# One of four states' inputs in the middle layers made by TensorE in two column tiles

## The chip, the cores and the metric

The kernel runs on one core of a Trainium2 chip. The metric is the time of one execution in device microseconds, as the median of several runs. Five engines work side by side, each with its own queue, in order: TensorE (PE in the profile; PEld is its weight load), VectorE (DVE), ScalarE (ACT), GpSimd (POOL) and SyncE (SP), which here issues the DMA transfers.

## The reference, cut to what matters

The network has four layers on images of 48 x 48 pixels with 192 channels, batch 4. Each rests on a selective scan over the 2304 pixels of an image: every channel has 16 states, and each state follows

```python
def step(h, t):
    d_t, u_t, b_t, c_t = t
    h = jnp.exp(d_t[..., None] * A) * h + (d_t * u_t)[..., None] * b_t[:, None, :]
    return (h, jnp.sum(h * c_t[:, None, :], axis=-1))
```

The factor `exp(d*A)` is called the decay here, `d*u` is called du, and `du*B` is what enters a state. The first layer (layer 0) and the last have 384 channels within. The two middle layers have 192 channels and four scans for each image: by rows, by columns, and both backwards. Their sum goes through a norm and, in the first of the two, a gate and a projection.

## The kernel before, in words

An image is cut into 6 chunks of 384 pixels. A *job* is one chunk of one direction of one image. In the middle layers (`ScanPools` with `parts=2`, jobs of class `DirJob`) the 192 channels lie in 3 blocks i of 64; the upper 64 partitions hold the same channels again with the other 8 of the 16 states. So a block has 8 states to a partition, in 2 groups g of 4 (`NG`). A job has 6 groups, and the number of a group in its job is called its *slot* here: even slots have g = 0. There are 2 layers x 4 directions x 4 images x 6 chunks = 192 jobs, and 1152 groups. Here is one group's way:

- `decay` (line 437): ACT computes four decays a, of 384 pixels each, two groups ahead of the scan. The buffer for a is one of three, so it waits for the scan of the group before the one now scanning.
- `fetch` (422): SP loads the rows of B and C of this group from HBM, repeated over the partitions, into a tile `bcb`.
- `drive` (465): POOL multiplies delta and x to du (tile `dus`), once per block. `enter` (470): ACT copies it to PSUM.
- `carry` (455): POOL copies the last state of the chunk before into one extra column of `bcb`, so that a scan over several states at a stretch starts each of them from it. That is why a row has 385 elements (`W`).
- `scan` (475): one DVE multiply, du times B of all four states (`inputs<-du,bcb`, 4 x 385 = 1540 elements), and one DVE scan over them (`h<-a,inputs`).
- `weigh` (501): POOL copies the last states out (`state<-h`) and multiplies h by C.
- `reduce` (516): TensorE sums the states into `y` (matmul records `y<-h,sum`), the lower and the upper half of the partitions going to two column tiles of 64.
- `take` (568), `gate` (572), `close` (577): ACT copies y out, TensorE adds its halves (`ps<-yc,sum`), ACT copies the result to `o`, and SP stores it.

Layer 0 and the last layer (`MambaJob`, `parts=1`) already have the form that the change brings to the middle layers. There, of the four states of a group, two (`MADE`) are not multiplied by DVE: TensorE makes du*B. For this a job writes B of these states to HBM and from there, one element of 4 bytes at a time, on the diagonals of 128 x 128 squares of zeros (`spread`, 641, tensors `be` and `dg`); `fetch` (662) loads them as part of `bcb`; `turn` (685) transposes du on TensorE and ACT copies it to `duT`; and `fill` (710) multiplies duT by the diagonal squares into the PSUM tile `made`. DVE then scans the made states straight from there (`h<-a,state,made` in layer 0, each state from its carried value).

The order of all this is written out in `run_jobs` (1029). At step t it queues the scan of group t, the decays of t+2, the weighing of t, the work of the next job that is due at this slot (`stream.run`: the projection to B, C and delta's input at slot 1, the three deltas at slot 2), the turn of t+2 if that is a block's first group, side work (the norms of finished images, in one job of four), the gate of t-3 if that was a block's last group, the drive of t+3, and the reduction of t-`behind`. Last comes `fill` of t+1. `behind` is 2 where TensorE makes inputs and 1 in the middle layers:

```python
        if 0 <= t - behind < len(groups) and behind == 1:
            job, i, g = groups[t - behind]
            job.reduce(i, g)
        if t + 1 < len(groups):
            job, i, g = groups[t + 1]
            job.fill(i, g)
```

Operations of DVE, POOL and TensorE that go through `InOrder` (51) and those of ACT (`in_order`, 106) keep this order; most transfers of SP are not bound to it. PSUM has 8 banks. In the middle layers before: four for `inputs`, one for du, one for y and two for `ps`, a pool of two buffers that projections, deltas, gates and side work use in turn.

Of the kernel before, what the change touches and what calls it, by code (L numbers as in the profile page):

```python
# [13 lines left out]
AF = mybir.ActivationFunctionType  # L14
# [7 lines left out]
Q = 96  # L22
# [6 lines left out]
MADE = 2  # L29
LINE = 3 * MADE * 128  # L30

# [30 lines left out]
class K:  # L62
# [100 lines left out]
    def mean_weights(self, n):  # L163
        w = self.tile(self.const, [Q, Q], f"mean{n}")
        self.nc.vector.memset(w, 1.0 / n)
        return w
# [82 lines left out]
class ScanPools:  # L249
# [6 lines left out]
    def __init__(self, k, ctx, parts, rows):  # L256
# [6 lines left out]
        self.made = parts == 1  # L263
# [9 lines left out]
        self.given = NG - MADE if self.made else NG  # L273
# [7 lines left out]
        if self.made:  # L281
            self.made_inputs = k.tile(self.vec, [128, 1024], "made")[:, 512 - CH : 512 + CH]
            self.n_jobs = 0
            self.diags = []
            zeros = self.decays[2].rearrange("p j l -> p (j l)")[:, : LINE + 1]
            k.g.memset(zeros, 0.0)
            for n in range(2 * self.groups):
                d = k.dram([128 * (LINE + 1)], "dg")
                k.nc.sync.dma_start(d.rearrange("(t x) -> t x", x=LINE + 1), zeros)
                self.diags.append(d)  # L290
# [41 lines left out]
class ScanJob:  # L332
# [16 lines left out]
    def turn(self, i):  # L349
        pass  # L350

    def turn_back(self, i):
        pass

    def fill(self, i, g):
        pass
# [55 lines left out]
    def spread(self):  # L412

        self.bc = self.k.dram([2 * N, self.pools.W], "bc")
        self.k.nc.sync.dma_start(self.bc, self.bcd[: 2 * N, :])
# [6 lines left out]
    def fetch(self, g):  # L422

        k, pools = self.k, self.pools
        wide = pools.wide
        both = k.tile(pools.bcs, [128, 2, NG, pools.W], "bcb")
        self.bcb[g] = both[:, 0, :, :], both[:, 1, :, self.tokens]
        self.fetched[g] = []
        for m in range(pools.parts):
            at = (m * pools.groups + g) * 2 * NG  # L430
            ins = k.nc.sync.dma_start(
                both[m * wide : (m + 1) * wide].rearrange("p s j l -> p (s j l)"),
                self.bc[at : at + 2 * NG, :].rearrange("r l -> (r l)").partition_broadcast(wide),
            )
            self.fetched[g].append(ins)

# [37 lines left out]

    def scan(self, i, g):

        k, pools = self.k, self.pools
        b, du, W = pools.b, pools.du, pools.W
# [3 lines left out]
        if pools.n_h >= pools.hbufs:  # L482
# [4 lines left out]
        k.v.tensor_tensor(  # L487
            b, du.unsqueeze(1).to_broadcast([128, NG, W]), self.bcb[g][0], ALU.mult
        )
        step = -1 if self.rev else 1  # L490
        h = self.h[i, g] = k.tile(pools.hs, [128, NG, W], "h")
        k.v.tensor_tensor_scan(
            h.rearrange("p j l -> p (j l)")[:, ::step],
            self.a.pop((i, g)).rearrange("p j l -> p (j l)")[:, ::step],
            b.rearrange("p j l -> p (j l)")[:, ::step],
            0.0,
            ALU.mult,
            ALU.add,
        )
# [36 lines left out]
class DirJob(ScanJob):  # L536
# [40 lines left out]
    def close(self, i):  # L577
        if i == 0:
            self.o = self.k.tile(self.pools.two, [64, 3, CH], "o")
        self.k.copy(self.o[:, i, :], self.ys)  # L580
        if i == 2:
            self.k.nc.sync.dma_start(self.part(self.dst), self.o)
# [5 lines left out]
class MambaJob(ScanJob):  # L588
# [52 lines left out]
    def spread(self):  # L641

        k, pools = self.k, self.pools
        sync = k.nc.sync
        n = pools.groups * (pools.given + NG)
        self.bc = k.dram([n, pools.W], "bc")
        sync.dma_start(self.bc, self.bcd[:n, :])
        be = k.dram([pools.groups, MADE, CH], "be")
        sync.dma_start(be.rearrange("g e l -> (g e) l"), self.bcd[n : 2 * N, self.tokens])
        at = pools.n_jobs % 2 * pools.groups  # L650
        pools.n_jobs += 1
        self.lines = pools.diags[at : at + pools.groups]
        for g in range(pools.groups):
            line = self.lines[g].rearrange("(t x) -> t x", x=LINE + 1)[:, :LINE]
            line = line.rearrange("t (b e c) -> t b e c", b=3, c=128)
            for e in range(MADE):
                with k.nc.allow_non_contiguous_dma(reason="diagonal"):
                    sync.dma_start(
                        line[:, :, e, 0:1], be[g, e].rearrange("(b t v) -> t b v", t=128, v=1)
                    )  # L660

    def fetch(self, g):

        k, pools = self.k, self.pools
        rows = pools.given + NG
        n = rows * pools.W
        t = k.tile(pools.bcs, [128, n + LINE], "bcb")
        both = t[:, :n].rearrange("p (j l) -> p j l", l=pools.W)
        self.bcb[g] = (
            both[:, : pools.given, :],  # L670
            both[:, pools.given :, self.tokens],
            t[:, n:].rearrange("p (b e c) -> p b e c", b=3, c=128),
        )
        ins = k.nc.sync.dma_start(
            t[:, :n],
            self.bc[g * rows : (g + 1) * rows, :]
            .rearrange("r l -> (r l)")
            .partition_broadcast(128),
        )
        k.nc.sync.dma_start(  # L680
            t[:, n:], self.lines[g][: 128 * LINE].rearrange("(t x) -> t x", t=128)
        )
        self.fetched[g] = [ins]

    def turn(self, i):

        k, pools = self.k, self.pools
        ps = k.tile(pools.ps, [128, 512], "ps")[:, :CH]
        self.turned_over(ps, self.du[i])
        self.duT[i] = k.tile(pools.two, [128, CH], "duT")  # L690
        k.copy(self.duT[i], ps)
        self.xd = k.tile(pools.one, [128, CH], "xd")
        k.act(self.xd, self.xs[:, i, :], AF.Identity, scale=self.w.D[:, i, :])
# [15 lines left out]

    def fill(self, i, g):  # L710

        k, pools = self.k, self.pools
        for b in range(3):
            at = slice(b * 128, (b + 1) * 128)
            for e in range(MADE):
                k.t.matmul(
                    pools.made_inputs[:, e * CH : (e + 1) * CH][:, at],
                    self.duT[i][:, at],
                    self.bcb[g][2][:, b, e, :],
                    start=True,  # L720
                    stop=True,
                    skip_group_check=True,
                )

    def scan(self, i, g):

        k, pools = self.k, self.pools
        waits = self.waits.pop((i, g))
        if g == 0:
            waits.append(pools.entered)  # L730
        if pools.n_h >= pools.hbufs:
            of = pools.n_h - pools.hbufs
            waits += [pools.readers[of], pools.weighed[of]]
        pools.n_h += 1
        k.gather(waits)
        n = pools.given
        du = pools.du.unsqueeze(1).to_broadcast([128, n, pools.W])
# [1418 lines left out]
```

## Time and profile before

| what | us |
|---|---|
| median of three runs (18009.92 to 18019.33) | 18016.76 |
| the profiled execution's own time | 18024.41 |
| its span, first to last instruction | 18022.6 |
| middle layers: first multiply of 1540 elements to last scan | 6085 to 12137 |
| DVE busy in the whole span | 16418.0 (91%) |
| TensorE busy in the whole span | 16243.2 (90%) |
| mean granted TensorE clock | 0.921 |

A line of the groups names the engine, the operation, out<-in by the tiles of the program, the shapes and the count; after the bar come busy time in us and the mean of one in ns, and after the second bar the idle time of the engine just before them with what ended it. A line of the timeline starts with its start and its duration in us; what stands in square brackets is the engine's idle time before it and what ended that. Records of one kind in a row are merged. An fp32 matmul is two records, each with its weight load; a transpose is one. A line of the windows gives a stretch, its length, the busy time of PE, PEld, DVE, ACT and POOL, each with the instructions in it, then the granted TensorE clock (1.00 is full speed), the mean share of the 16 DMA engines and GB/s.

### The profile page before, as it was taken

To read this page: it belongs to the slowest core of one execution; us is meant where nothing else is said; L and a number is where in the kernel's file an instruction comes from. 1 tells how busy PE (TensorE), PEld (TensorE's weight loads), DVE (VectorE), ACT (ScalarE), POOL (GpSimd) and SP (SyncE) were. 2 spreads that over 40 slices of the span, in tenths; PEclk is the share of its full clock that TensorE was granted. 3 is DMA by queue.
4 is the path that set the end of the run, shared out by engine and by line. 5 is a ranking of instruction groups with operands and counts; after the bars stand their busy time and mean duration, and the time that the engine had idled before them with its cause. 6 is when DMAs were issued, how large, how long until landed. Compare 5 with 4: busy or idle time off the path is not lost. (4 is left out here: it accounts for less than half of the span.)

```text
span 18022.6 us, 313028 instructions
## 1 busy us (share of the span) xinstructions
PE 16243.2 (90%) x118512; PEld 10759.8 (60%) x118512; DVE 16418.0 (91%) x10747; ACT 13776.3 (76%) x25601; POOL 14149.0 (79%) x10862
## 2 busy tenths in 40 slices
PE   9999999999999777787777877878999999999999
PEld 7787787888885322222222222226888888888874
DVE  8899899999996799999999999996999999999992
ACT  7888888888885567777777777777888888888874
POOL 7877878878874488888888888876888888888880
PEclk9999999999999878788888887789999999999999
DMA  4343343333333466666666666663343343433431
GB/s 137 122 128 124 125 134 122 128 126 128 128 126 93 105 137 146 151 148 153 152 148 149 144 150 140 147 145 112 122 127 125 120 124 123 132 123 122 125 118 50
DMA packets 1229187, 2324.58 MB, mean 129 GB/s; under 512 B 704376, under 2 KB 962016, under 8 KB 1075232
## 3 DMA queue, kind: packets, MB, share of 16 engines
q1 hardware_dynamic: 1227680, 2304.55, 46.8%
q8 instruction: 938, 15.37, 0.4%
q14 instruction: 569, 4.66, 0.1%
HBM read 2105.57 MB, written 200.98 MB: 128 GB/s over the span
## 5 line engine op out<-in xcount | busy, mean ns | idle before, releaser
L59 POOL TENSOR_TENSOR h<-h,bcb 128x1536 f32<-128x1536 f32 x3456 | 11312.2, 3273 | 798.6 <-DVE h L59 499.1
L104 ACT ACTIVATE a<-delta,A 128x384 f32<-128x384 f32 (+1 forms) x13824 | 7377.6, 603 | 911.7 <-DVE h L59 901.2
L59 DVE TENSOR_TENSOR_SCAN h<-a,inputs 128x770 f32<-128x770 f32 (+2 forms) x3456 | 7915.9, 2290 | 146.5 <-DVE inputs L59 1.8
L59 DVE TENSOR_TENSOR inputs<-du,bcb 128x770 f32<-128x770 f32 (+2 forms) x3456 | 4256.4, 1232 | 287.2 <-POOL bcb L59 100.9
L59 PE MATMUL made<-bcb,duT 128*128 128x128 f32 x27648 | 3559.6, 279 | 172.1 <-DVE h L59 139.6
L59 PEld LDWEIGHTS y<-ident,h 128*128 128x128 f32 x27648 | 3119.8, 142 | 845.0 <-issue 485.7
L59 PE MATMUL y<-ident,h 128*128 128x128 f32 x27648 | 3508.5, 277 | 59.8 <-ACT yt L104 49.2
L59 PEld LDWEIGHTS made<-bcb,duT 128*128 128x128 f32 x27648 | 3341.4, 195 | 273.9 <-DVE h L59 178.7
L59 PE MATMUL y<-h,sum 128*64 128x384 f32 x9216 | 2661.7, 643 | 750.2 <-POOL h L59 547.4
L59 DVE TENSOR_TENSOR_SCAN h<-a,made 128x768 f32<-128x768 f32 (+1 forms) x1536 | 2343.2, 1536 | 263.2 <-PE made L59 256.4
L59 PEld LDWEIGHTS y<-h,sum 128*64 128x64 f32 x9216 | 848.7, 167 | 2175.9 <-issue 982.2
L59 DVE TENSOR_TENSOR_SCAN h<-a,state,made 128x384 f32<-128x384 f32 x1920 | 1827.8, 993 | 221.1 <-PE made L59 219.4
L59 POOL COPY state<-h 128x4 f32<-128x4 f32 x2304 | 434.4, 189 | 1908.5 <-DVE h L59 1879.5
L59 PE MATMUL ps<-bcd,dtT 12*128 12x384 f32 (+1 forms) x2304 | 1076.9, 580 | 245.1 <-ACT delta L104 240.2
L59 PE MATMUL ps<-u,inT 96*128 96x384 f32 x3456 | 1251.7, 489 | 38.8 <-DMA u<-xn_wh 27.1
L104 ACT ACTIVATE delta<-ps,vec 128x384 f32<-128x384 f32 x1152 | 636.4, 577 | 344.3 <-PE ps L59 338.2
L59 PEld LDWEIGHTS ps<-bcd,dtT 12*128 12x128 f32 (+1 forms) x2304 | 415.1, 206 | 808.8 <-ACT delta L104 487.3
L59 PE MATMUL ps<-yt,outT 128*96 128x384 f32 x2304 | 808.7, 488 | 0.4 <-POOL yt L59 0.4
L59 PE MATMUL ps<-xh,diag 32*32 32x192 f32 x32256 | 796.8, 324 | 4.0 <-ACT xc L104 2.3
L59 PEld LDWEIGHTS ps<-u,inT 96*128 96x128 f32 x3456 | 600.5, 191 | 304.0 <-issue 36.4
L104 ACT ACT_TABLE_LOAD x603 | 773.6, 1283 | 10.6
L101 ACT ACT_TABLE_LOAD x600 | 769.8, 1283 | 9.8 <-PEq L2146 0.7
(147 smaller groups left out, 15082.7 us busy)
## 6 DMA issues: line engine op xcount, KB each, us to landing
bcb<-bc SPq DMA_DIRECT2D x768, 770.0 KB
bcb<-bc SPq DMA_DIRECT2D x384, 1155.0 KB
bcb<-bc SPq DMA_DIRECT2D x384, 1152.0 KB
bcb<-dg SPq DMA_DIRECT2D x768, 384.0 KB
y<-o SPq DMA_DIRECT2D x192, 288.0 KB
xs<-xi_wh SPq DMA_DIRECT2D x96, 288.0 KB
xs<-xi_hw SPq DMA_DIRECT2D x96, 288.0 KB
added<-y SPq DMA_DIRECT2D x96, 288.0 KB
```

What stands on the lines that cost most here:

```text
L59: return lambda *a, **kw: self.tc.keep_in_program_order(op(*a, **kw))
L101: self.in_order(self.nc.scalar.preload_act_table_set(LOG_EXP))
L104: return self.in_order(self.nc.scalar.activation(out, in_, func, **kw))
```

## The change

In the middle layers DVE now multiplies three of a group's four states. TensorE makes the fourth: for each of three pixel blocks of 128 and each half m of the partitions, one matmul of duT (128 pixels x 64 channels) with that half's diagonal square, into the half's own column tile of `made`. DVE scans three states as before and then the fourth from `made`, with the carried state as the scan's first value. `spread`, `fetch`, `turn`, `fill` and `scan` move from `MambaJob` to the common class, and `MADE` becomes a table by `parts`. In PSUM `inputs` gives one bank to `made`. `o` gets one buffer instead of two, and the weights `mean96` move to the pool of the stage that uses them. `behind` stays 2 for the outer layers and 1 for the middle ones (`turned`). Rows of the projection are put in another order to match.

```diff
-MADE = 2
-LINE = 3 * MADE * 128
+MADE = {1: 2, 2: 1}
...
-        self.made = parts == 1
+        self.made = MADE[parts]
+        self.turned = parts == 1
+        self.line = 3 * self.made * parts * 128
...
-        self.given = NG - MADE if self.made else NG
+        self.given = NG - self.made
...
+        made = k.tile(self.vec, [128, 512 * self.made], "made")
...
     def spread(self):
...
+        self.bc = k.dram([n, pools.W], "bc")
+        sync.dma_start(self.bc, self.bcd[:n, :])
+        be = k.dram([parts, pools.groups, made, CH], "be")
+        sync.dma_start(be.rearrange("m g e l -> (m g e) l"), self.bcd[n : 2 * N, self.tokens])
...
+        for g in range(pools.groups):
...
+            for e in range(made):
+                for m in range(parts):
+                    with k.nc.allow_non_contiguous_dma(reason="diagonal"):
+                        sync.dma_start(
+                            line[:, :, e, m, 0:1],
+                            be[m, g, e].rearrange("(b t v) -> t b v", t=128, v=1),
+                        )
...
     def fetch(self, g):
...
+        k.nc.sync.dma_start(
+            t[:, n:], self.lines[g][: 128 * pools.line].rearrange("(t x) -> t x", t=128)
+        )
...
+    def turn(self, i):
+
+        k, pools = self.k, self.pools
+        wide = pools.wide
+        ps = k.tile(pools.ps, [128, 512], "ps")[:, : 3 * wide]
+        for b in range(3):
+            k.t.matmul(
+                ps[:, b * wide : (b + 1) * wide],
+                self.du[i][:wide, b * 128 : (b + 1) * 128],
+                k.ident[:wide, :wide],
+                start=True,
+                stop=True,
+                is_transpose=True,
+                skip_group_check=True,
+            )
+        self.duT[i] = k.tile(pools.two, [128, 3, wide], "duT")
+        k.copy(self.duT[i].rearrange("p b d -> p (b d)"), ps)
+
+    def fill(self, i, g):
+
+        k, pools = self.k, self.pools
+        wide = pools.wide
+        for b in range(3):
+            for e in range(pools.made):
+                at = e * CH + b * 128
+                for m in range(pools.parts):
+                    k.t.matmul(
+                        pools.made_inputs[m * wide : (m + 1) * wide, at : at + 128],
+                        self.duT[i][:, b, :],
+                        self.bcb[g][2][:, b, e, m, :],
+                        start=True,
+                        stop=True,
+                        skip_group_check=True,
+                    )
...
     def scan(self, i, g):
...
+        scan(slice(0, n), slice(0, pools.W), pools.b.rearrange("p j l -> p (j l)"))
+        if pools.rows:
+            scan(slice(n, NG), self.tokens, pools.made_inputs)
+            return
+        for e in range(pools.made):
+            at = g * NG + n + e
+            first = 0.0 if self.prev is None else self.prev.state[:, i, at : at + 1]
+            scan(
+                slice(n + e, n + e + 1),
+                self.tokens,
+                pools.made_inputs[:, e * CH : (e + 1) * CH],
+                first,
+            )
...
     def close(self, i):
         if i == 0:
-            self.o = self.k.tile(self.pools.two, [64, 3, CH], "o")
+            self.o = self.k.tile(self.pools.one, [64, 3, CH], "o")
...
-    behind = 2 if jobs[0].pools.made else 1
+    behind = 2 if jobs[0].pools.turned else 1
```

## The prediction

> **What bounds the kernel now.** I first split the page's span by stage. The widths of DVE's two costliest groups tell the layers apart: 1540 elements is only in the middle layers, whose first multiply starts at 6085 us and whose last scan ends at 12137. The groups of instructions with shapes kept apart, over the whole span (mean ns after the busy time):
>
> ```profile
> L59 DVE TENSOR_TENSOR_SCAN h<-a,inputs 128x1540 f32<-128x1540 f32 x1152 | 3871.8, 3361 | 43.9 <-DVE inputs L59 0.5
> L59 DVE TENSOR_TENSOR inputs<-du,bcb 128x1540 f32<-128x1540 f32 x1152 | 2039.1, 1770 | 121.0 <-POOL bcb L59 28.4 <-ACT a L104 20.8 <-ACT du L104 16.7
> L59 DVE TENSOR_TENSOR_SCAN h<-a,inputs 128x770 f32<-128x770 f32 x1152 | 2024.0, 1757 | 41.9
> L59 DVE TENSOR_TENSOR_SCAN h<-a,state,made 128x384 f32<-128x384 f32 x1920 | 1827.8, 993 | 221.1 <-PE made L59 219.4
> L59 DVE TENSOR_TENSOR inputs<-du,bcb 128x770 f32<-128x770 f32 x1152 | 1109.1, 963 | 108.5 <-POOL bcb L59 72.5 <-ACT a L104 35.0 <-DMA bcb<-bc 0.4
> ```
>
> The last three are layer 0, where two of four states are already made by TensorE. Then the stage's busy times (order PE, weight load, DVE, ACT, POOL; then granted clock, DMA share, GB/s):
>
> ```profile
> 6085.00:12137.00 6052.00, 4710.49 (x14794) 1606.17 (x14794) 5907.75 (x2304) 4399.31 (x8193) 5026.89 (x4282) 0.80 0.65 147
> ```
>
> DVE is busy for 5908 of 6052 us: it is the bound, at 5.20 us a group (its multiplies start at 9020.51, 9025.71, 9030.91). But TensorE, at 0.80 of its clock, has its work spread round waits, so last I read one job's timeline engine by engine. A job is six groups, "slots" 0 to 5; slot 2 starts at 9020.51:
>
> ```profile
> 9020.54 1.55 PE L59 MATMUL ps<-bcd,dtT 12*128 12x384 f32 x4
> 9024.59 1.64 PE L59 MATMUL ps<-bcd,dtT 12*128 12x384 f32 x2 [2.50 <-ACT delta L104]
> 9026.17 0.90 PE L59 MATMUL ps<-yc,sum 128*64 128x384 f32 x1
> ...
> 9026.87 3.39 PE L59 MATMUL y<-h,sum 128*64 128x384 f32 x7
> ```
> ```profile
> 9020.51 2.13 ACT L104 ACTIVATE a<-delta,A 128x384 f32<-128x384 f32 x4 [1.16 <-DVE h L59]
> 9022.66 1.28 ACT L104 ACT_TABLE_LOAD   x1
> 9023.96 1.05 ACT L104 ACTIVATE delta<-ps,vec 128x384 f32<-128x384 f32 x2
> 9026.27 0.58 ACT L104 ACTIVATE delta<-ps,vec 128x384 f32<-128x384 f32 x1 [1.26 <-PE ps L59]
> ```
> ```profile
> 9000.01 3.44 POOL L59 TENSOR_TENSOR h<-h,bcb 128x1536 f32<-128x1536 f32 x1
> 9003.42 1.00 POOL L59 TENSOR_TENSOR dus<-delta,xs 128x384 f32<-128x384 f32 x1
> ```
>
> The first two show slot 2: TensorE stands 2.50 us for ACT's deltas, and the reduction of slot 1's states ends only at 9030.26, 9.75 us after the slot began. The third is slot 4 (start 8999.71): the next du is there 4.71 us into the slot. Today all this hides: with four h buffers a late reduction stops nobody.
>
> **DVE's gain.** Per group, a multiply and a scan of 1540 become 1155, half way between the rows: (963+1770)/2 = 1367 ns and (1757+3361)/2 = 2559 ns. The made state's scan is new: 993 ns (row). The gap per instruction is (5.20-5.13)/2 = 0.035. New group: 1.367+2.559+0.993+0.105 = 5.024, saving 0.176; x1152 = 203 us. In 32 of 192 jobs there is no carried state; such a scan averages 935 in layer 0, so 192 x 0.058 = 11 us more. Gain 214 us, if the made values are never late.
>
> **What the made values wait for.** `fill(t+1)` writes the one `made` bank, so it can't start until DVE's last scan of t ends; and TensorE's queue, in order, holds it behind `turn`, `gate` and `reduce(t-1)`, since `behind` stays 1 here. DVE needs it at 5.02 + 1.37 + 2.56 + 0.07 = 9.02 us after slot t's start. If it is late, DVE stops at the made scan, and behind that stand the next group's multiply, POOL's weighing and ACT's decays (which want the freed buffer). Nothing gives the stall back.
>
> Durations: gate and reduce together 2.12 us at full clock (9000.36 to 9002.48), 4.09 at half (9026.17 to 9030.26). Turn: three transposes, 0.49 in layer 0, 0.8 at half clock. Fill: 12 records. Unoverlapped, layer 0's twelve take 1.50 us; if the two column tiles overlap, half, 0.75. Page "TensorEngine Tiling (Array Packing)", Theoretical Speedup, allows up to 2x for a side of 64. The row half agrees: eight half-width records of 384 take 1.51, four full-width (u,inT) 1.46. But weight loads of `y<-h,sum` are busy 848.7/9216 = 92 ns each, twelve make 1.1. I take 1.1 at full clock, 1.6 at half (ends 0.75 and 3.0).
>
> *Slots 0 and 4.* Turn is queued ahead of gate and waits for du: 4.71+0.05. At full clock +0.49+2.12+1.1 = 8.47, cover 0.55. At half clock +0.8+4.09+1.6 = 11.25, late by 2.2.
>
> *Slot 2.* PSUM's two `ps` buffers now also serve turn, so gate gets the third delta's buffer and waits for ACT to read it: 9026.85 instead of 9026.17, 6.34 into the slot. Then 4.09+1.6: 12.03, late by 3.0. At full clock (one job's third delta ended at 5.60): 5.60+2.12+1.1 = 8.82, just in time.
>
> So the clock decides. Page "TensorE: Matmul & The Clock Gate", Part 1 (HAM oscillation), says that only idle gaps above about 3.4 us throttle. By it the 2.50 us gap leaves TensorE at speed and the kernel gains 214 us. The trace differs (same columns as the stage's line; the clock is third from the end):
>
> ```profile
> 9022.10:9024.60 2.50, 0.01 (x1) 0.01 (x1) 2.47 (x2) 2.47 (x5) 2.50 (x3) 0.79 0.00 0
> 9024.60:9026.20 1.60, 1.60 (x4) 0.52 (x4) 1.56 (x2) 0.41 (x1) 1.14 (x4) 0.50 0.12 31
> 9026.20:9030.30 4.10, 4.07 (x11) 1.25 (x10) 4.07 (x2) 4.00 (x7) 3.38 (x2) 0.50 0.98 213
> ```
>
> Counted over all jobs, the clock 5 to 8 us into slot 2 averages 0.53 to 0.63, and the reduction ends at a median of 9.44, already past 9.02 before fill is added. I take the row: 9.44+0.68 for gate's buffer+1.6 = 11.7, late 2.7; with a few jobs at full clock 2.5. For slots 0 and 4 the clock there averages 0.85 to 0.97, but turn now stands ahead, so TensorE idles some 3 us first; I take half clock in 3 of 10: 0.3 x 2.2 = 0.66, two slots 1.3. In 48 jobs side work (four `ny,center` records, 1.53 us) goes ahead of gate in slots 0 and 4; it overdraws the 0.55 by 1.0, twice: 48x2x1.0/192 = 0.5 per job. Odd slots: no turn, weighing ends at 3.75, cover 2 us: none.
>
> Sum: (2.5+1.3+0.5) x 192 = 826 us lost, 214 gained: +612.
>
> **The other edits.** *ACT:* three duT copies a job, at most 0.49 each; ACT is busy 73%, in slot 2 it follows the deltas, off gate's path: 0. *SP:* per job five more issues before fetch (be, four scatters at 0.625, layer 0's `dg<-be`) and two `bcb<-dg` at 0.43. bc is issued near 3.8 us into slot 2 (9024.30); with be's landing and the scatters' (estimated 2.5 each) the fetch goes out about 12 us after slot 2 began, lands near 16.6, and POOL's carry of the next job wants it at about 18.8 (3.7 into slot 5). Cover 2 us: 0, else POOL stands with the weighing behind it. The loads of xs and the store of o, also SP's, have a slot to spare. *DMA:* 786 KB of lines a job in, 394 KB of B rows out, on 4.6 MB: share 0.65 to about 0.71; hidden. *o in one buffer:* stored from 8999.91, rewritten at 9007.73: covered. *POOL:* carry copies 3 columns, not 4: 0; its weighing takes 3.44 here but 2.91 in layer 0, for reasons the trace doesn't show: if the new tile brings it to 2.91, slots 0 and 4 gain 0.53 of cover, slot 2 nothing; I keep 3.44. *Zero lines, `mean96`:* once, under 5 us. Outer layers: same instructions.
>
> **Rivals and numbers.** The sum stands against the profiled span, 18022.6 us (its run 18024.4), which is 7.6 over the median 18016.8; +612 on the median gives 18629.
> - *Fill late, mainly in slot 2* (chance 0.78): 18090 to 19190. Low end: only slot 2, late by 1.5: 288-214 = +74. High end: slot 2 at 3.0, the others at 1.3 each, side 0.6: 6.2x192-214 = +976, and up to 190 for a late fetch or unoverlapped fills.
> - *The clock stays up* (0.12): fills keep TensorE busy through today's gaps, slot 2 meets 8.82, and 214 us come back, less some side work: about 17830. It decides once slot 2's clock is near 1.0. For it: layer 0, with fills, shows 0.98. Against: slot 2's gap is ACT's, and its 12-row matmuls before and after it didn't bring the clock back.
> - *Near even* (0.04): slot 2 late by about 1.1 and nothing else: 1.1x192-214 = -3, 18014.
> - *Half clock in all three even slots, fills unoverlapped* (0.06): 3x3.2x192-214 = +1630, 19650.
>
> The range, 18000 to 19200, takes in the first and third case and leaves out the other two, 0.18. Within 0.2%, 36 us, is what a measurement of this kernel can't tell from no change. Faster 0.12, same 0.04, slower 0.84.
>
> **What the profile will show.** Right: DVE idle before `h<-a,made` in the middle stage, released by PE `made`, about 800 us in all, most after slot 2; groups of 1367, 2559 and 993 ns. Wrong: little such idle time with slot 2's clock near 1.0; or the idle time released by a DMA or POOL; or weighing at 2.91.

## The result, and the profile after

The changed kernel takes 18808.8 us (median of four runs, 18785.98 to 18816.29) against 18016.18 us of the kernel before in the same session: ratio 1.0438, 95% interval 1.042 to 1.0456. It is 793 us slower; the forecast was 612 slower. All of it is in the middle layers: their stage, from the first multiply to the last scan, grew from 6052 to 6851 us.

The groups of DVE instructions inside that stage, changed kernel (busy us and mean ns after the bar, then idle time ahead of them and what ended it):

```profile
L58 DVE TENSOR_TENSOR_SCAN h<-a,inputs 128x1155 f32<-128x1155 f32 x1152 | 2948.3, 2559 | 43.4
L58 DVE TENSOR_TENSOR inputs<-du,bcb 128x1155 f32<-128x1155 f32 x1152 | 1573.0, 1365 | 355.2 <-POOL bcb L58 248.6 <-DMA bcb<-bc 73.1 <-POOL state L58 5.4
L58 DVE TENSOR_TENSOR_SCAN h<-a,state,made 128x384 f32<-128x384 f32 x960 | 962.0, 1002 | 721.2 <-PE made L58 720.3
L58 DVE TENSOR_TENSOR_SCAN h<-a,made 128x384 f32<-128x384 f32 x192 | 180.8, 942 | 191.2 <-PE made L58 190.7
```

The stage's line of busy times, same columns as before:

```profile
6085.00:12936.00 6851.00, 5556.16 (x30358) 2699.73 (x30359) 5562.19 (x3456) 4497.41 (x8766) 5026.88 (x4284) 0.86 0.63 141
```

DVE's largest wait in the stage, and TensorE's (what waited, what ended it; us in total, times, longest):

```profile
DVE h L58 <- PE made L58: 911.0, 542, 5.2
```
```profile
PE ps L58 <- POOL dus L58: 722.3, 311, 4.6
```

Three things are to be read here. DVE's own work fell from 5908 to 5562 us, and the granted clock of TensorE rose from 0.80 to 0.86; both speak for the change. But DVE now stands 911 us for the values that TensorE makes, which it never did in this stage before, and 322 us (248.6 + 73.1) for the rows of B, against 31 before; a wait put down to POOL's `bcb` is the carry, which itself waits for the load. The sum is -346 + 911 + 290 = +855. Other waits of DVE came to 39 us less than before, and gaps that no wait explains to 18 us less, which makes +798, against +799 measured for the stage. TensorE's 722 us are `turn` waiting for du, 295 us in slots 0 and 419 in slots 4, with gate, reduce and fill behind it in the queue.

One job shows both waits. TensorE's timeline in slot 2, which starts at 9057.98:

```profile
9063.59 0.40 PE L58 MATMUL ps<-ident,dus 64*128 64x64 f32 x3
9064.33 0.54 PE L58 MATMUL ps<-yc,sum 128*64 128x384 f32 x1 [0.34 <-ACT delta L103]
...
9065.89 0.64 PE L58 MATMUL made<-bcb,duT 128*64 128x128 f32 x2
9066.42 0.85 PE L58 MATMUL y<-h,sum 128*64 128x384 f32 x1
9067.06 1.49 PE L58 MATMUL made<-bcb,duT 128*64 128x128 f32 x10
```

and DVE's timeline over slots 2 and 3, and in slots 0 and 1 of the next job:

```profile
9061.85 0.99 DVE L58 TENSOR_TENSOR_SCAN h<-a,state,made 128x384 f32<-128x384 f32 x1
9063.01 1.36 DVE L58 TENSOR_TENSOR inputs<-du,bcb 128x1155 f32<-128x1155 f32 x1 [0.16 <-POOL bcb L58]
9064.41 2.56 DVE L58 TENSOR_TENSOR_SCAN h<-a,inputs 128x1155 f32<-128x1155 f32 x1
9068.60 1.01 DVE L58 TENSOR_TENSOR_SCAN h<-a,state,made 128x384 f32<-128x384 f32 x1 [1.64 <-PE made L58]
...
9080.07 1.37 DVE L58 TENSOR_TENSOR inputs<-du,bcb 128x1155 f32<-128x1155 f32 x1
...
9088.95 1.37 DVE L58 TENSOR_TENSOR inputs<-du,bcb 128x1155 f32<-128x1155 f32 x1 [3.94 <-DMA bcb<-bc]
```

The bank is free from 9062.84 (9061.85 + 0.99), but fill stands behind gate and reduce: its first two records start at 9065.89, while the last of reduce are still under way, its other ten at 9067.06, and it ends at 9068.55. DVE's made scan, due at 9066.96, starts 1.64 us late. Gate waits for ACT's third delta because turn has taken its `ps` buffer, and starts 6.35 us into the slot. The prediction had 6.34; over all jobs the median is 7.1. The granted clock falls just there:

```profile
9060.00:9064.50 4.50, 3.24 (x19) 1.50 (x16) 4.30 (x4) 3.94 (x7) 4.42 (x6) 1.00 0.04 3
9064.50:9069.00 4.50, 4.04 (x22) 2.16 (x20) 2.87 (x2) 4.47 (x8) 2.26 (x2) 0.62 0.60 141
```

The second wait, 3.94 us at 9088.95, comes from SP's queue in the same slot 2:

```profile
9063.57 0.54 SPq L414 DMA_DIRECT2D bc<-bcd  x1
9064.17 0.28 SPq L416 DMA_DIRECT2D be<-bcd  x1
...
9066.97 2.59 SPq L426 DMA_DIRECT2D dg<-be  x4
9069.67 1.20 SPq L451 DMA_DIRECT2D bcb<-bc  x2
...
9073.14 1.60 SPq L451 DMA_DIRECT2D bcb<-bc  x2
```

The first group's rows are issued at 9069.67, 11.7 us into slot 2 (predicted: about 12). The second group's are issued at 9073.14, behind them in one burst, and the wait for them ends at 9088.9: 16 us after issue, 31 us into the slot.

Over all jobs, by the medians of the trace's DMA packets, counted from the start of slot 2: the first load goes out at 9.1 us and the last packet of the second group's rows ends at 28.5; in the kernel before it was 5.4 and 23.3. In between 3.7 MB move in 18 us, against 3.9 MB in 18 us before. So the burst isn't larger than it was; it starts 3.7 us later.

Over all 192 jobs, the wait for made falls on the slot whose scan is late as follows: slot 0 69 us, slot 1 95, slot 2 51, slot 3 380, slot 4 82, slot 5 234. Of the 322 us for rows, 257 are in slot 1.

### The profile page after: what moved, and what is told of

The parts are those of the page before. It is cut to its first block, busy times and chain, and to the rows that moved or that the text cites. A ratio compares the mean times of both kernels' runs of the same rounds, so it can differ in the third digit from the quotient of the medians.

```text
span 18808.1 us, 347232 instructions
## 1 busy us (share of the span) xinstructions
PE 17085.5 (91%) x134064; PEld 11850.1 (63%) x134064; DVE 16069.9 (85%) x11899; ACT 13874.4 (74%) x26177; POOL 14145.6 (75%) x10863
## 5 line engine op out<-in xcount | busy, mean ns | idle before, releaser
L103 ACT ACTIVATE a<-delta,A 128x384 f32<-128x384 f32 (+1 forms) x13824 | 7373.6, 603 | 21.6 <-DVE h L58 12.4
L58 DVE TENSOR_TENSOR_SCAN h<-a,inputs 128x770 f32<-128x770 f32 (+2 forms) x3456 | 6993.1, 2023 | 146.0 <-DVE inputs L58 1.4
L58 PE MATMUL made<-bcb,duT 128*128 128x128 f32 (+1 forms) x41472 | 4906.6, 287 | 254.6 <-DVE h L58 140.4
L58 PEld LDWEIGHTS made<-bcb,duT 128*128 128x128 f32 (+1 forms) x41472 | 4428.4, 181 | 905.1 <-issue 534.1
L58 DVE TENSOR_TENSOR inputs<-du,bcb 128x770 f32<-128x770 f32 (+2 forms) x3456 | 3790.8, 1097 | 526.5 <-POOL bcb L58 319.9
L58 DVE TENSOR_TENSOR_SCAN h<-a,state,made 128x384 f32<-128x384 f32 x2880 | 2790.3, 996 | 941.9 <-PE made L58 939.7
L58 DVE TENSOR_TENSOR_SCAN h<-a,made 128x768 f32<-128x768 f32 (+1 forms) x1728 | 2524.6, 1470 | 445.0 <-PE made L58 437.6
L103 ACT ACTIVATE duT<-ps 128x384 f32<-128x384 f32 (+1 forms) x1152 | 469.9, 408 | 1692.4 <-PE ps L58 1691.1
L58 PE MATMUL ps<-ident,dus 64*128 64x64 f32 (+1 forms) x3456 | 538.8, 268 | 763.7 <-POOL dus L58 722.3
L58 PE MATMUL ps<-bcd,dtT 12*128 12x384 f32 (+1 forms) x2304 | 972.9, 529 | 136.6 <-ACT delta L103 132.1
L58 PEld LDWEIGHTS ps<-ident,dus 64*128 64x128 f32 (+1 forms) x3456 | 376.4, 148 | 982.2 <-POOL dus L58 820.9
```

What stands on the lines that cost most here:

```text
L58: return lambda *a, **kw: self.tc.keep_in_program_order(op(*a, **kw))
L103: return self.in_order(self.nc.scalar.activation(out, in_, func, **kw))
```

## The experiments

The theory to be tested: the loss is the order of TensorE's queue (fill stands behind gate and reduce) and, beside it, loads that are issued late behind the scatters. The rivals: the loss is TensorE's clock; the late loads come from a larger burst, or from something else ahead of them on SP's queue; TensorE is simply full. Ratios are against the kernel before on the same chip, with their 95% intervals.

**Fill ahead of gate and reduce.** In the middle layers fill(t+1) is issued right after the projections of the slot:

```diff
         stream.run(at if at < per - 1 else per)
+        if behind == 1 and t + 1 < len(groups):
+            job, i, g = groups[t + 1]
+            job.fill(i, g)
```

> Only TensorE's queue order in the middle layers changes: fill(t+1) stands right behind the next job's projections and deltas, ahead of turn, gate and reduce(t-1). Nothing else, and the same work. Theory Q (the made values are late because fill is queued last): fill can start when DVE's last scan of t ends, or in slot 2 when the third delta is through (about 5.7 us into the slot), and is due about 8.8: DVE's 907 us of waiting for made in the stage fall below 150, the waits on bcb stay near 320; about 18050 us. Rival K (the half clock alone makes the chain too slow, wherever fill stands): the waiting falls by less than half, and the time stays above 18350.

Measured: 18755.6 us, ratio 1.0415 (1.04 to 1.0431). DVE's waits in the stage, then ACT's:

```profile
DVE inputs L58 <- ACT du L103: 775.0, 348, 6.9
DVE inputs L58 <- POOL bcb L58: 205.5, 122, 4.5
...
DVE h L58 <- PE made L58: 63.3, 68, 1.9
```
```profile
ACT duT L103 <- PE ps L58: 1488.2, 569, 13.0
```

Made is no longer late, so the place was right; but the time came back as a wait for `du`. Fill waits for DVE to leave the bank, turn now stands behind fill, ACT's copy of duT waits for turn, and behind that copy stands `enter`, which hands du to DVE. The stall had moved, not gone, and the time is far from the 18,050 expected.

**No scatters.** Leaves out the copy to `be` and the four scatters of a job; the diagonals stay zero, so the fourth state receives nothing. The loads keep their bytes.

```diff
-        sync.dma_start(be.rearrange("m g e l -> (m g e) l"), self.bcd[n : 2 * N, self.tokens])
+        if parts == 1:
+            sync.dma_start(be.rearrange("m g e l -> (m g e) l"), self.bcd[n : 2 * N, self.tokens])
...
-        for g in range(pools.groups):
+        for g in range(pools.groups if parts == 1 else 0):
```

> Leaves out, in the middle layers, the store of the made rows (be) and the four scatters onto the diagonals, so that the lines stay zero and the fourth state of each group gets nothing; the loads of the lines and all of TensorE's work stay. Theory L (the new waits of DVE on bcb, 321 us in the stage against 31 before, come from the fetch that must wait for be and the scatters and then sends both groups' loads at once): those waits fall below 80, waits for made stay within 100 of 907; 18500 to 18560 us. Rival P (POOL's carry is late because the whole group chain is late): the waits on bcb stay above 250, time within 60 of 18809.

Measured: 18650.1 us, 1.0351 (1.0336 to 1.0367). DVE's waits:

```profile
DVE h L58 <- PE made L58: 992.5, 579, 6.7
DVE inputs L58 <- POOL bcb L58: 58.7, 165, 1.1
DVE inputs L58 <- DMA bcb<-bc: 23.9, 2, 22.4
```

The waits for rows fall from 322 to 83 us, so the scatter path makes the loads late: the first load goes out at 5.6 us into slot 2 instead of 9.1, and the second group's rows are there at 22.1 instead of 28.5 (medians). One thing more changed with it: with no scatter to wait for, the load of one group's diagonals goes out ahead of the burst. The time falls by 159, not 239: the waits for made grew by 81, as slack that the one stall gave was used up by the other.

**No fill.** Leaves out turn, the copy of duT and fill (`made` is set to zero once):

```diff
+        if parts == 2:
+            k.nc.vector.memset(made, 0.0)
...
     def turn(self, i):
+        if pools.parts == 2:
+            return
...
     def fill(self, i, g):
+        if pools.parts == 2:
+            return
```

> Leaves out turn, its copy and fill in the middle layers: made is set to zero once and the fourth state of each group gets nothing; DVE's instructions and the loads are those of the changed kernel. Measures what DVE gains alone. If a group costs DVE the 4.80 to 4.88 us from start to start that undisturbed groups of the changed kernel show, the stage comes to 1152 x 4.85 = 5590 us plus the waits on bcb (300): about 17850 us. If it were the 5.02 that I summed from the rows, about 18100 us. Theory L also expects the waits on bcb to stay (over 200 us); rival P expects them gone with the late made values (under 80).

Measured: 18248.5 us, 1.0131 (1.0114 to 1.0148). DVE's waits:

```profile
DVE inputs L58 <- POOL bcb L58: 467.0, 226, 5.7
DVE inputs L58 <- DMA bcb<-bc: 72.7, 24, 6.0
```

Even with TensorE's part gone the kernel is slower than before, and 400 us slower than the 17,850 expected. Late rows alone, 540 us where 300 were expected, are more than the 237 us between this kernel and the one before.

**Dummy matmuls to hold the clock up.** First into a spare part of `made` (six ahead of the third delta, ten ahead of turn in slots 0 and 4), then, since these waited for DVE on that tile, into the `ps` tile that is overwritten next (six ahead of the second delta, ten ahead of turn):

```diff
+    def keep_warm(self, ps, n):
+        for _ in range(n):
+            k.t.matmul(ps[:, :128], k.ident, k.ident, start=True, stop=True, skip_group_check=True)
...
+        if pools.parts == 2 and i != 2:
+            self.keep_warm(ps, 10)
```

> Adds matmuls that nobody reads: six before the third delta of a job (where TensorE waits for ACT in slot 2) and ten before turn in slots 0 and 4 (where it waits for du). Theory K (the half clock is what makes fill late): the clock of the stage rises from 0.86 to above 0.95, DVE's 907 us of waiting for made fall to 300 to 500; 18250 to 18450 us. Theory Q without the clock (order and waits for ACT decide, whatever the clock): waiting for made stays above 750 or rises, since the added matmuls stand in the same queue; 18750 us or more.

> The added matmuls once more, now into the ps tile that the next operation overwrites, so that they wait for nothing of DVE: six before the second delta, ten before turn in slots 0 and 4. Theory K (half clock makes fill late): clock of the stage above 0.94, waiting for made from 907 to 300 to 550, 18250 to 18500 us. Theory Q (order and the waits for ACT and POOL, whatever the clock): waiting for made stays above 750, 18650 us or more.

Measured: 19363.5 us, 1.0751 (1.0735 to 1.0767), for the first: its waits for made are 1668 us, because the dummies, which share a tile with fill, stood waiting for DVE (571 us of TensorE's time ahead of work on `made`, 6 in the changed kernel); it tells nothing of the clock. For the second: 18836.6 us, 1.0455 (1.0439 to 1.047). Its stage line and its first wait:

```profile
6085.00:12947.00 6862.00, 6227.22 (x40307) 3699.06 (x40309) 5565.85 (x3456) 4493.98 (x8777) 5029.79 (x4284) 0.94 0.63 141
```
```profile
DVE h L58 <- PE made L58: 1063.1, 622, 4.3
```

The clock rose from 0.86 to 0.94. From gate to the end of fill it took a median of 2.8 us instead of 4.5 in slot 2 and 2.8 instead of 4.1 in slot 4. But gate started later, behind the dummies (8.1 instead of 7.1 us into slot 2, 7.6 instead of 5.4 into slot 4), fill ended later too (11.3 instead of 10.9, 10.4 instead of 9.7), and the time didn't fall. A higher clock bought with work in the same queue is worth nothing here; what a higher clock at no cost would give stays open.

**Turn, fill, gate, reduce.** As the first experiment, but with turn kept ahead of fill in TensorE's queue:

```diff
         if soon := at_group(t + 2, 0):
             soon[0].turn(soon[1])
+        if behind == 1 and t + 1 < len(groups):
+            job, i, g = groups[t + 1]
+            job.fill(i, g)
```

> Only TensorE's queue order changes again: turn, then fill(t+1), then gate and reduce(t-1). In the run with fill ahead of turn, DVE's waiting for made was gone, but ACT stood at its copy duT behind that fill, and DVE then waited 777 us for ACT's du. Theory Q: with turn in front, duT is copied about 5.3 us into an even slot and fill is through by 6.2 (slot 2: 8.1), due 8.8: waiting for made below 120, for ACT's du below 120, and the waits on bcb stay at 300 to 540 (the run without fill had 540): 18200 to 18350 us. Rival K (half clock): in slot 2 fill still ends after 8.8 in most jobs, waiting for made above 300, 18450 us or more.

Measured: 18560.5 us, 1.0303 (1.0285 to 1.032), the fastest so far of those that compute everything, and short of what was expected. DVE's waits:

```profile
DVE inputs L58 <- ACT du L103: 470.6, 277, 4.6
DVE inputs L58 <- POOL bcb L58: 261.3, 192, 4.8
DVE h L58 <- PE made L58: 106.7, 99, 3.9
```
```profile
PE made L58 <- DMA bcb<-dg: 429.2, 179, 6.6
```

The waits for du fall to 471 us only, 178 of them in slots 2 and 274 in slots 4. The last line is TensorE's, and new with fill moved up: in slots 0 and 1 it now stands 429 us for the load of the diagonals, the last of the late burst (436 us in the first experiment, 82 in the changed kernel). It is not what makes du late: in the 129 jobs in which TensorE stood over 0.3 us for the diagonals, DVE waits 2.6 us a job for du, in the other 63 2.2.

**The zero column by ACT.** The column of zeros at the entry of `bcd` was set by POOL, whose queue held a weighing ahead of it; ACT writes it instead, alone and together with the order just described:

```diff
-                k.g.memset(self.bcd[:, self.entry : self.entry + 1], 0.0)
+                e = self.bcd[:, self.entry : self.entry + 1]
+                if pools.parts == 2:
+                    k.act(e, px[:, 0:1], AF.Copy, scale=0.0)
```

> The changed kernel with ACT instead of POOL writing the zero column of bcd in the middle layers, nothing else. Theory L: waits on bcb fall from 321 to below 120, but the waits for made rise by about 100 as they did without the scatter (the stall that is taken away upstream is partly met again at made): about 18640 us. Rival B: 18780 us or more.

> As the order turn, fill, gate, reduce, and ACT instead of POOL writes the zero column of bcd in the middle layers (bcd times 0, one column), so that SP's store of bc no longer waits for POOL's weighing and the be, scatter and fetch chain starts about 4 us sooner. Theory L (late start of the fetch): the waits on bcb fall below 120, the group comes near the 4.85 us of DVE: 17700 to 17850 us, faster than both kernels. Rival B (bandwidth: the 390 KB more per job are the cause, not the start): waits on bcb stay above 250, 18000 us or more.

Measured: alone 18794.5 us, 1.0434 (1.0418 to 1.0449); with the order 18557.4, 1.0303 (1.0287 to 1.0318), the same as without it. The waits for rows stay at 251 and 306 us (322 and 320 without the edit). POOL's zero was not what made the loads late.

**Turn one group before its use.** Turn is issued in the odd slots, where du is two slots old, and fill behind it:

```diff
-        if soon := at_group(t + 2, 0):
-            soon[0].turn(soon[1])
+        if soon := at_group(t + behind, 0):
+            if t or behind == 2:
+                soon[0].turn(soon[1])
+        if behind == 1 and t + 1 < len(groups):
+            job, i, g = groups[t + 1]
+            job.fill(i, g)
```

> In the middle layers the turn is issued one group ahead of its use and not two: in slots 1, 3 and 5, where du was made two slots earlier, so nothing on TensorE, or on ScalarE's copy of duT behind it, waits for GpSimd; the fill follows the turn at once, ahead of gate and reduce. Theory Q (the loss is work standing in the wrong order, and each earlier reordering only moved the stall to ScalarE's copy of duT): waits for made stay near 110 us, those for du fall from 471 to below 150, those of late loads stay at 300 to 450; the time falls from the 18,560 of the order turn, fill, gate, reduce to 18,150 to 18,300. Rival K (what counts is the clock that TensorE gets and the work added to it): waits for du go elsewhere, time stays within 1% of 18,560.

Measured: 18704.4 us, 1.0392 (1.0372 to 1.0411), slower than with turn two groups ahead. TensorE's waits and DVE's:

```profile
PE made L58 <- ACT duT L103: 562.1, 457, 4.6
PE made L58 <- DMA bcb<-dg: 465.5, 151, 12.1
```
```profile
DVE inputs L58 <- ACT du L103: 573.5, 273, 5.2
DVE inputs L58 <- POOL bcb L58: 278.1, 178, 5.4
DVE h L58 <- PE made L58: 169.3, 183, 4.2
```

Now TensorE, at fill, stands for ACT's copy of duT and nearly as long for the diagonals, and gate and reduce stand behind fill; ACT's `enter` is late as before, presumably because gate's result comes late to ACT in its turn; that last link was read from the order and not tried. A third place for the same stall. The expectation had counted only POOL and TensorE and had left out that turn directly ahead of fill puts ACT's queue between them.

**Scatters straight from SBUF.** On top of that, without the copy to `be`:

```diff
-                            be[m, g, e].rearrange("(b t v) -> t b v", t=128, v=1),
+                            self.bcd[row : row + 1, self.tokens].rearrange("o (b t) -> o b t", t=128),
```

> As e10_turn_odd, and the four scatters of a job read the fourth state's rows straight from the tile in SBUF: the copy to be and the wait of about 2.2 us for its landing are gone from the queue of SyncE in the middle layers, the rows and the scatters are the same. Theory L (the second group's rows come late because the loads are issued late, behind the wait and the scatters): the waits of late loads fall by half, from 300 to 450 to about 150, and the time by 150 to 250 us against e10_turn_odd, which could bring it near or just below the kernel before (17,950 to 18,150). Rival B (they are late because the burst of loads itself is larger by the diagonals' tiles): no difference over 60 us from e10_turn_odd.

Measured: 19111.6 us, 1.0609 (1.0594 to 1.0625), 407 us slower than its base. SP's instructions on the diagonals, ns min/median/max, in this kernel and then in the changed kernel:

```profile
L436 SPq DMA_DIRECT2D dg<-bcd x764: 722/1263/2586, 6099.1 to 13176.9; - x191
```
```profile
L426 SPq DMA_DIRECT2D dg<-be x788: 530/624/1709, 6107.4 to 13197.9; - x197
```

An issue of a scatter whose source is a row in one partition of SBUF holds SP for 1.26 us, twice the 0.62 from HBM. The edit also takes the elements in another order, so source and order aren't told apart. The wait for `be` was gone: the scatters begin at 5.1 us into slot 2 instead of 8.8 (medians). But they end at 11.2, where they ended at 11.4; the first load goes out at 11.4 instead of 10.1, the second group's rows are there at 29.8 instead of 27.6, and the waits for rows rose from 345 to 621 us. The idea that a shorter path to the scatters brings the loads forward stands untested by this run, since the path was not shorter.

**No fill and no scatters.** Leaves out both, with the edits of those two runs together; DVE's three instructions and all loads stay.

> Leaves out in the middle layers both the turn, the copy of duT and the fill (made's tile is set to zero once) and the copy to be with the scatters (the diagonals' lines stay zero); VectorE's three instructions and all loads stay. It gives what VectorE alone gains. With the gain of 0.35 to 0.40 us per group that undisturbed groups show (4.8 against 5.2), 1152 groups give 17,580 to 17,620 plus what late loads are left; the prediction's 0.176 us per group would give 17,810. Expected 17,650 to 17,750. If late loads stay over 200 us without any scatter, the rival B of the larger burst holds, and the time is near 17,900.

Measured: 17671.6 us, 0.9813 (0.9798 to 0.9827), as expected. Stage line and DVE's waits:

```profile
6085.00:11804.00 5719.00, 4560.23 (x14802) 1573.64 (x14803) 5506.24 (x3456) 4366.51 (x8192) 5013.44 (x4283) 0.82 0.72 168
```
```profile
DVE inputs L58 <- POOL bcb L58: 53.8, 130, 2.0
```

This is what the change gives on DVE when next to nothing that feeds it is late: 340 us. Beside the run without fill alone, the copy to `be` and the scatters ahead of the loads cost 577 us, and the waits for rows fall from 540 to 55 us. The first load goes out at 5.6 us into slot 2 instead of 8.2, and the second group's rows are there at 21.6 instead of 26.3 (medians). So 2.6 of these 4.7 us are the later start. The other 2 are a longer burst, since here too one load of diagonals goes out ahead of it (16.1 us from first issue to last packet, against 18.2). The scatters as the cause are shown; the burst is not cleared by this pair of runs, but by the kernel before, where it was as long.

**Half of the reduce.** The order turn, fill, gate, reduce, with a reduce that sums only two of a group's four states (the other two are left out of the output), to take from TensorE about what turn and fill gave it:

```diff
-        for j in range(NG):
+        for j in range(2 * g, 2 * g + 2) if parts == 2 else range(NG):
```

> As e7_turn_fill (order turn, fill, gate, reduce), and the reduce of the middle layers sums two of a group's four states (two matmuls of 384 columns in the place of four; the other two states are left out of the sum). That takes some 1.2 us of TensorE per group (two records at the 0.57 to 0.61 us that they are busy in the profile), about what turn and fill added (1.4 us). Theory C (TensorE is simply full: after the change it is busy 4.81 us per group at a granted clock of 0.85, and VectorE needs 4.80, so each order only chooses who waits): the waits for made and du, 585 us together in e7_turn_fill, fall below 200, and the time from 18,560 to 17,950 to 18,150, with late loads of 250 to 350 us left. Rival O (the order of ScalarE's and TensorE's queues, waits on single instructions at fixed places): the waits stay above 400, the time above 18,350.

Measured: 18642.0 us, 1.0352 (1.0335 to 1.0369): not faster than its base of 18560.5 but slower by 0.4%. TensorE's groups in the stage, this kernel and then its base, and DVE's waits in this kernel:

```profile
L58 PE MATMUL y<-h,sum 128*64 128x384 f32 x4604 | 1867.0, 646 | 69.6 <-ACT yc L103 68.4
L58 PE MATMUL made<-bcb,duT 128*64 128x128 f32 x13824 | 1461.8, 348 | 795.4 <-DMA bcb<-dg 398.0 <-DVE h L58 266.5 <-ACT a L103 43.5
```
```profile
L58 PE MATMUL y<-h,sum 128*64 128x384 f32 x9202 | 2452.5, 565 | 75.3 <-ACT yc L103 73.5
L58 PE MATMUL made<-bcb,duT 128*64 128x128 f32 x13812 | 1231.3, 308 | 768.2 <-DMA bcb<-dg 429.2 <-DVE h L58 214.4 <-ACT a L103 55.1
```
```profile
DVE inputs L58 <- ACT du L103: 422.8, 262, 6.6
DVE inputs L58 <- POOL bcb L58: 275.0, 187, 5.5
DVE h L58 <- PE made L58: 184.5, 156, 5.5
```

Half of the reduce's records are gone, but its busy time falls only from 2452 to 1867 us, and the records got longer (reduce 565 to 646 ns, fill 308 to 348): the granted clock fell from 0.88 to 0.77 in the stage. The test was weaker than meant, since TensorE's busy time fell by 3% only (5387 to 5231 us). Still, 4600 matmul records fewer moved no wait away (607 us for du and made, 577 before): no sign that the amount of TensorE's work decides, though with the lower clock the rival isn't ruled out.

## Why the prediction was right, and which terms were off

The direction and the main mechanism were right: made values come late, because fill is queued last, and that costs more than DVE gains. The measured 18808.8 lies in the range and in the likeliest case's own range. The total is nearer than its terms: a gain that was too small and a loss put at nothing offset each other in part, which is luck. By its steps:

- **DVE's gain** was mis-sized. The rows were right to 1% (1367, 2559 and 993 ns forecast; 1365, 2559 and 1002 or 942 measured), but the sum of a group, 5.024 us, was not: the prediction added three gaps of 0.035 us, read where each instruction needs what the one before it uses. The multiply and the scan of one `inputs` tile keep that gap. But a made scan behind the scan of `inputs` needs nothing of it, nor does the next multiply need the made scan, and both start before the other's end. In the job shown, the scan at 9059.38 lasts 2.56, and the made scan starts at 9061.85, 0.09 ahead of its end. Undisturbed groups take 4.79 us. Layer 0 of the kernel before shows the same overlaps (3002.51 + 1.76 is 3004.27, and 3004.19 + 1.89 is 3006.08):

```profile
3002.51 1.76 DVE L59 TENSOR_TENSOR_SCAN h<-a,inputs 128x770 f32<-128x770 f32 x1
3004.19 1.89 DVE L59 TENSOR_TENSOR_SCAN h<-a,state,made 128x384 f32<-128x384 f32 x2
3006.01 0.96 DVE L59 TENSOR_TENSOR inputs<-du,bcb 128x770 f32<-128x770 f32 x1
```

  DVE's busy time shows a gain of 402 us without late made values (5908 to 5506, no fill and no scatters), of which 340 reach the kernel's time, and 346 in the changed kernel, where late scans lose the overlap; forecast 214.
- **Fill late**, forecast 826 us, measured 911. For slot 2 (whose late scan is slot 3's) 480 was forecast and 380 measured; for slots 0 and 4 with the side work 346 and 329, of which slot 4 has 234. The remaining 202 us come from the fills of the odd slots, to which the prediction gave no loss ("cover 2 us: none").
- **Fetch late**, put at 0 for a cover of 2 us, measured about 290 us more than before. This is the step that failed. Its time of issue fits the job shown (11.7 against about 12 us into slot 2; the median is 9.1). But it gave the first load 4.6 us to land, where 10 us pass from issue to last packet already in the kernel before (medians, 5.4 to 15.3). And it left out the second group's rows, which go out behind the first's and land last; DVE stands for them in slot 1. With the same step "*DMA:* hidden" fails: the mean share of 0.65 hides that the engines are full during the burst (1.00 from 9031.8 to 9046.0 in the kernel before).
- **"So the clock decides"** is not supported. The prediction took half clock in slot 2, and 0.85 to 0.97 in slots 0 and 4 with half in 3 of 10. In the changed kernel the means over all jobs, 5 to 8 us into the slot, are 0.72 to 0.92 in slot 2, 0.62 to 0.76 in slot 4 and 0.78 to 0.83 in slot 0. The stage's clock rose to 0.86 and the kernel is slower; with 0.94, bought by dummies, it is no faster, and with 0.77 (half of the reduce) only 0.4% slower than at 0.88. Fill ahead of gate and reduce took the waits for made from 911 to 63 us at a clock of 0.89, so the order decides who waits. The Trainium skill, "TensorE: Matmul & The Clock Gate", Part 1 (HAM oscillation), gives as its rule that TensorE should have no idle gaps above about 3.4 us. This case's trace differs: in the middle layers of the kernel before, the clock fell from full to half 359 times, and in 311 of them TensorE's longest idle time in the 4 us before was shorter than that. So the row was the better guide, and weighing it against the page led to the right side; that the clock was the cause is not shown by it.
- **Terms at nothing.** *ACT's duT copies:* right in this order (2 us of waits for du); with fill moved up, waits for du become the longest (775, 471 and 574 us). *POOL's weighing:* 3.44 kept, 3.45 measured. *o in one buffer:* "covered" was not quite so; ACT stood 91 us for the store (48 times), with nothing on DVE put down to it.
- **The last rival's sum** is too small by its own terms: with fills of 3.0 at half clock the even slots would be late by 3.6, 4.4 and 3.6 us, not by 3.2 each. It didn't come, since two column tiles overlap.

The balance of causes: fill gone alone gives 560 us (18808.8 to 18248.5), scatters gone alone 159, both 1137. The two stalls hide one another, so neither alone shows its price.

What stays open: whether a second `made` bank would end the chain DVE, fill, DVE. The kernel's eight banks of PSUM are taken (three for `inputs`, one each for du, `made` and y, two for `ps`), and it wasn't tried. Nor was another queue for the scatters, nor the order turn, fill, gate, reduce without the scatters, which would show what the order is worth once the loads are on time. Three orders of TensorE's queue were tried besides the change's own; in each the waits for made fell and waits for du, behind ACT, took their place, and none came within 3% of the kernel before.

## What to carry to other kernels

When work moves to an engine that looks 20% idle, follow every queue that its operands pass, and not the engine's share: here each group gained a round DVE, TensorE, DVE through one bank and, per block, a second through ACT, and wherever fill was put, something else stood behind it. A step that adds small DMAs delays whatever stands behind them on the issuing queue: cost the last load of the burst, not the first, with the DMA share of that burst and not of the whole stage. Read gaps between instructions from a place with the same dependences. And measure a ceiling early: leaving out both feeders at once showed 340 us to be won, while leaving out either alone showed a kernel still slower than before.

## What the runs showed of the hardware

- DVE instructions overlap where the later one needs nothing of the earlier: 0.08 to 0.09 us behind a scan. Where it reads or overwrites the same `inputs` tile, a gap of 0.03 us stays. Rows of 1365, 2559 and 989 ns, together 4.91 us, so run every 4.79 us.
- Twelve fill records (128x128, two column tiles of 64) take 0.82 to 0.88 us at full clock when nothing stands between them, where layer 0's twelve over all 128 columns take 1.50: the two tiles overlap. The prediction had bounded them by 0.75 and 3.0 and taken 1.1 to 1.6.
- TensorE's granted clock was higher in the runs in which TensorE was busy for more of the stage: 0.80 before (busy 0.78 of it), 0.86 after (0.81), 0.94 with the dummies (0.91), and 0.76 and 0.82 in the two runs without fill (0.77 and 0.80). Taking away half of the reduce lowered it from 0.88 to 0.77; what was taken from TensorE came back in part as slower matmuls.
- A scatter of 384 elements of 4 bytes holds SP for 0.62 us when it reads HBM and for 1.26 us when it reads one partition of SBUF, in another order of elements.
